# The first stage of a transformer block: x and the condition's weights in larger transfers, the modulation computed ahead of the first transposes

## The chip, the cores and the metric

The kernel runs on one core of one Trainium2 chip. The metric is the time of one execution in device microseconds (us), lower is better. Two more numbers are told apart from it: the span, from the first to the last instruction of one profiled execution, and the time of that same execution, which is a little longer than its span.

## The reference, cut to what matters

One block with adaptive modulation: 2 rows of 2048 tokens, 512 features, 16 heads of 32, hidden size 2048, all in float32. The condition (2 x 512) makes six vectors per row, which shift, scale and gate.

```
mod = silu(condition) @ Wada + bada
sh_a, sc_a, gt_a, sh_m, sc_m, gt_m = split(mod, 6)
xn = layernorm(x) * g1 + be1
xm = xn * (1 + sc_a) + sh_a
x = x + gt_a * attention(xm, Wqkv, Wproj, bproj)       # causal
xn = layernorm(x) * g2 + be2
xm = xn * (1 + sc_m) + sh_m
x = x + gt_m * (gelu(xm @ W1 + b1) @ W2 + b2)
```

## The kernel before, in words

**Stages.** For each of the two rows: a stage that makes q, k and v (class Qkv, pool names qkv0 and qkv1), then attention (attention_phase). The projection of the first row's attention runs in project_phase together with the beginning of the second row's q/k/v stage. The MLP over all tokens ends the kernel. The change edits the beginning of the first row's q/k/v stage, and three methods that both rows use: load_x, and through Qkv.run the order of stats and scaled.

**The q/k/v stage.** A row is cut into 4 groups (g) of 512 tokens, a group into 4 tiles of 128 tokens (MTT = 4). For each group x is loaded (load_x, line 915), each tile's mean and variance are taken by VectorE (stats, L218 bn_stats and L221 bn_aggr), ScalarE takes the square root (L224), VectorE inverts it and makes shift = -mean/std (L225, L226), and ScalarE scales each tile in place (scaled, L964). A pair of tiles (half a group, j = 0 or 1) is then transposed by TensorE (transposed, L214, eight transposes of 128x128 into two PSUM banks), and VectorE (L269) and ScalarE (L274) apply the modulation on the way out into xmT. The products use one level of a seven-product scheme (Strassen's, in the form of Winograd). For each block f of 128 columns of q and k, and then for two blocks of the values, a unit issues the products a(A11), b(S1), a(S2), b(S4), c(A12), a(S3), and, after the first two steps of the next unit, a(A22). Several products add to one PSUM bank, and ScalarE (L1059) or VectorE (L1072, L1078) must copy or subtract a bank's value before the next product is added to it. GpSimd (POOL) makes the sums of weights that the scheme needs (weight_sum L944, value_weight_sums L949), VectorE the sums of tokens (L997). The first block of the first group is done without the scheme (plain: 8 matmuls of 128x512, ps_qk), so that it does not wait for those sums. q and k are split in two parts each (hi on ScalarE L1064, lo minus hi on VectorE L1066, in later groups on POOL) and stored to scratch memory by SyncE (SP, L1031).

**The order around the steps.** Qkv.run counts steps (n, 42 per group); at step 3 it asks for the next group's x if it is not there, at steps 10 to 13 it takes its statistics, at 15 and 25 it scales its tiles in pairs, at 18 and 28 it transposes them, and at 30 it asks for the x after that. From group 1 on, scores of the attention (tile s, with their maxima on VectorE, L498 and L504) are mixed into the steps. A scheduler then orders each engine's instructions; those wrapped in act(), mm() or transpose() keep their program order on their engine, the others may be moved. stats takes a flag keep, which wraps its bn_stats in act(). So a flag here can move other instructions of VectorE and ScalarE too.

**The beginning of the first row** (lines 1360 to 1474). ScalarE issues seven small transfers, cond, g1, be1, g2, be2, b1 and b2, into one tile rows of 44 rows. SP issues x of group 0 (4 transfers of 128x512), the two blocks of Wada for shift and scale (load_wada, 8 transfers of 128x512 into room borrowed from the value tile vv), the q/k weights wqk (4 of 128x2x512) and the value weights wv (4 of 128x2x256). TensorE transposes rows (ps_c), VectorE copies it to cols, ScalarE makes silu of the condition's columns into sc (L1457). modulation(0) is 8 matmuls (ps_mod) of 32 columns of weights each, in four column strips of the array; its columns() adds the bias, brings the result into columns by 4 small matmuls (ps_modt) and copies it to mod; scale_shift makes a1 and c1 from it, with which the transposed tiles are modulated. In the program the first pair of tiles is transposed ahead of modulation(0), the second behind it. ScalarE needs one set of tables for Sqrt and another for Silu, and loads them when it changes from one to the other.

x tiles have 4 buffers; a new x waits until its buffer's last tile is scaled and transposed.

Of the kernel before, what the change touches and what calls it, by code (L numbers as in the profile page):

```python
# [17 lines left out]
P = 128  # L18
# [9 lines left out]
def dit_block_kernel(  # L28
# [106 lines left out]
    first = const.tile([P, 1], F32, tag="first", name="first")  # L135
    nc.scalar.activation(first, eps, AF.Sqrt)

# [760 lines left out]
    class Qkv:  # L898
# [16 lines left out]
        def load_x(self, g):  # L915
            xts = []
            for t in range(MTT):
                xt = self.qp.tile([P, D], F32, tag="x", name="x", bufs=4)
                nc.sync.dma_start(xt, x_rows(self.row.b * NT + g * MTT + t))
                xts.append(xt)  # L920
            self.xts[g] = xts
# [216 lines left out]
        def run(self, hp, also, early=()):  # L1138
# [3 lines left out]
            for g in range(NG):  # L1142
                at = [0]

                def tick():
# [5 lines left out]
                    if g + 1 < NG:  # L1151
                        if n == 3 and g + 1 not in self.xts:
                            self.load_x(g + 1)
                        if 10 <= n < 10 + MTT and g + 1 > row.b:
                            self.stats(g + 1, n - 10)
                        if n in (15, 25):
                            self.scaled(g + 1, n // 25)
                        if n in (18, 28):
                            self.norm(g + 1, n // 28)()
                        sums = {36: S1, 38: S2, 40: S3}  # L1160
                        if n in sums:
                            self.token_sum(g + 1, sums[n])
# [199 lines left out]
    with pool("wada") as wp, pool("qkv0") as qp, pool("hl0") as hp, pool(  # L1362
        "ps_qkv0", bufs=6, space=PSUM
    ) as ps_mm:
        rows = wp.tile([n_rows, P], F32, tag="rows", name="rows")
        for r, n, src in (
            (0, n_cond, cond.rearrange("b (c p) -> (b c) p", p=P)),
# [5 lines left out]
            (r_b2, C, b2.rearrange("(c p) -> c p", p=P)),  # L1373
        ):
            nc.scalar.dma_start(rows[r : r + n, :], src)
        wada_v = Wada.rearrange("(c p) f -> p c f", p=P)
        wada = {}

        def load_wada(s0, s1):
# [6 lines left out]
            for n, s in enumerate((s0, s1)):  # L1386
# [3 lines left out]
                )  # L1390
            for k in range(C):
                for n, s in enumerate((s0, s1)):
                    nc.sync.dma_start(w[:, n, k, :], wada_v[:, k, s * D : (s + 1) * D])
            wada[s0] = w, mr
# [47 lines left out]
        def scale_shift(a, c, r_g, r_be, shift, scale):  # L1442
# [13 lines left out]
        act(  # L1456
            nc.scalar.activation(  # L1457
                sc[:, :, :B], col(0, n_cond).rearrange("p (b c) -> p c b", c=C), AF.Silu
            )
        )  # L1460
# [15 lines left out]
        def also(g, n):  # L1476
# [852 lines left out]
```

## Time and profile before

| | us |
|---|---|
| median of 3 runs | 2249.56 (2248.82 to 2253.02) |
| the profiled execution: its time | 2252.46 |
| its span | 2250.7 |
| TensorE idle within the span | 40.6 |
| start of the first q/k matmul (ps_qk) | 18.28 |
| start of the first product by the scheme (ps_a) | 26.95 |
| granted TensorE clock, mean over the span | 0.999 |

Views used below: the page, the chain that ended last (start, length, engine, tile and line of each piece, in order of time), windows (busy time of each engine in a stretch, granted clock, share of the DMA engines' time, GB/s), and the timeline (start, length, engine, line, operation, tiles, shapes, count; in brackets the idle time before it and what ended it). PE is TensorE's matmuls, PEld its weight loads, DVE VectorE, ACT ScalarE, SPq the issue of transfers on SyncE. A float32 matmul is two records in the trace, a transpose one.

### The profile page before, as it was taken

What the parts mean: (1) busy time and instruction counts of PE and PEld (TensorE: products, weight loads), DVE (VectorE), ACT (ScalarE), POOL (GpSimd) and SP (SyncE); (2) the same over time, 40 slices, a digit from 0 to 9 for tenths busy, and PEclk for the clock granted to TensorE, in tenths of its full rate; (3) what the DMA queues carried; (4) which work ended last, traced back from release to release, by engine and by line L of the source; (5) the groups of instructions that cost most, each with busy time, mean ns of one, the idle gap of its engine ahead of it and who ended that gap; (6) DMA issues with size and microseconds to landing.
All of it is one profiled execution on the core that took longest, in us unless ns stands there. A gap on an engine that the chain in (4) does not pass through costs nothing.

```text
span 2250.7 us, 33467 instructions
## 1 busy us (share of the span) xinstructions
PE 2210.1 (98%) x12057; PEld 1429.4 (64%) x12057; DVE 1537.3 (68%) x3309; ACT 1003.6 (45%) x2012; POOL 1298.3 (58%) x807
## 2 busy tenths in 40 slices
PE   7999999999999999999999999999999999999998
PEld 5887555555543588855555555345787787688687
DVE  4678766777757667777677767663685585576576
ACT  4434555555564253365665556614322422331410
POOL 4253998998983696299989898444105204304210
PEclk9999999999999999999999999999999999999999
DMA  8787142231324799532324113363353354353433
GB/s 274 247 277 193 44 92 70 62 85 48 107 96 135 247 308 321 152 83 67 80 67 104 48 46 131 108 233 127 114 174 131 125 182 147 106 187 126 159 126 109
DMA packets 160510, 311.57 MB, mean 138 GB/s; under 512 B 16544, under 2 KB 48844, under 8 KB 158552
## 3 DMA queue, kind: packets, MB, share of 16 engines
q1 hardware_dynamic: 155488, 285.53, 41.8%
q0 software_dynamic: 4480, 23.36, 2.7%
q8 instruction: 95, 1.56, 0.3%
q14 instruction: 71, 0.58, 0.1%
q10 hardware_dynamic: 376, 0.55, 0.1%
HBM read 229.95 MB, written 87.29 MB: 141 GB/s over the span
## 4 chain that ended last, share of the span: by engine, by line
PE 88%; DVE 4%; POOL 3%; DMA 2%; ACT 1%; issue 1%; SPq 0%; DVEq 0%; ACTq 0%; POOLq 0%
PE ps_a L206 26%; PE st L206 18%; PE ps_b L206 12%; PE o L206 10%; PE s L206 9%; PE ps_c L206 4%; PE sm L206 3%; PE ps_o L206 3%; DVE junk L498 1%; POOL ee L695 1%; PE ps_xt L214 1%; ACT e L670 1%; DVE mx L504 1%; PE ps_o L214 1%; DVE stat L218 1%
## 5 line engine op out<-in xcount | busy, mean ns | idle before, releaser
L670 ACT ACTIVATE e<-st 128x512 f32<-128x512 f32 (+1 forms) x1152 | 575.1, 579 | 362.6 <-PE st L206 319.2
L504 DVE TENSOR_REDUCE mx<-s 128x1 f32<-128x512 f32 x576 | 381.6, 686 | 193.4 <-PE s L206 192.4
L695 POOL TENSOR_TENSOR ee<-ee,e 128x2048 f32<-128x2048 f32 x106 | 485.8, 4583 | 10.4 <-ACT e L670 4.4
L206 PE MATMUL st<-qst,kst 128*128 128x512 f32 (+3 forms) x1280 | 408.8, 386 | 0.0
L206 PE MATMUL s<-kst,qst 128*128 128x512 f32 (+3 forms) x1046 | 380.5, 395 | 6.1 <-DVE mx L504 3.7
L206 PE MATMUL ps_a<-sum,w 128*128 128x256 f32 (+1 forms) x1088 | 328.7, 431 | 0.1
L206 PE MATMUL o<-e,vv 128*32 128x512 f32 (+3 forms) x2560 | 293.2, 537 | 0.3 <-POOL e L682 0.3
L206 PEld LDWEIGHTS st<-qst,kst 128*128 128x128 f32 x1280 | 228.5, 188 | 97.7 <-issue 66.0
L498 DVE CUSTOM_DVE_ANT_0 junk<-s,causal 128x128 bf16<-128x128 f32 (+3 forms) x470 | 220.7, 470 | 61.0 <-PE s L206 47.0
L1797 POOL TENSOR_TENSOR sum<-w 128x256 f32<-128x256 f32 x30 | 22.1, 738 | 395.2 <-PE ps_a L206 263.8
L206 PEld LDWEIGHTS s<-kst,qst 128*128 128x128 f32 x1046 | 194.9, 188 | 71.1 <-DVE mx L504 17.0
L206 PEld LDWEIGHTS ps_a<-sum,w 128*128 128x128 f32 x1088 | 204.5, 190 | 40.1 <-issue 11.4
L695 POOL TENSOR_TENSOR ee<-e 128x2048 f32<-128x2048 f32 x42 | 192.5, 4583 | 43.2 <-ACT e L670 42.3
L206 PEld LDWEIGHTS <-sel 32*128 32x128 bf16 x1152 | 29.5, 91 | 197.0 <-issue 196.1
L2016 ACT ACTIVATE h<-h,cols 128x512 f32<-128x512 f32 x120 | 76.8, 711 | 136.0 <-DVE h L1718 136.0
L504 DVE TENSOR_REDUCE mx<-st 128x1 f32<-128x512 f32 x192 | 131.0, 683 | 0.6
L682 POOL TENSOR_SCALAR_AFFINE_SELECT e<-e 128x512 f32<-128x512 f32 x128 | 83.3, 669 | 67.6 <-ACT e L670 67.5
L206 PE MATMUL st<-fold,sel 32*128 32x512 bf16 (+1 forms) x1152 | 117.5, 372 | 1.3
L206 PEld LDWEIGHTS o<-e,vv 128*32 128x32 f32 x2560 | 59.1, 108 | 92.4 <-issue 73.0
L1718 DVE TENSOR_TENSOR h<-c,ps_b 128x256 f32<-128x256 f32 x90 | 37.9, 421 | 103.5 <-PE ps_b L206 103.0
L1066 POOL TENSOR_TENSOR lo<-lo,hi 128x512 fp32r<-128x512 f32 x32 | 40.6, 1274 | 103.9 <-ACT hi L1064 102.0
L206 PE MATMUL ps_b<-sum,w 128*128 128x256 f32 (+1 forms) x384 | 95.0, 383 | 0.0
(237 smaller groups left out, 3590.2 us busy)
## 6 DMA issues: line engine op xcount, KB each, us to landing
qst<-q SPq DMA_DIRECT2D x128, 256.0 KB
kst<-k SPq DMA_DIRECT2D x128, 256.0 KB
w<-w1d SPq DMA_DIRECT2D x32, 896.0 KB
w<-w2d SPq DMA_DIRECT2D x28, 1024.0 KB
w<-w2d SPq DMA_DIRECT2D x28, 768.0 KB
q<-hi SPq DMA_DIRECT2D x32, 256.0 KB
q<-lo SPq DMA_DIRECT2D x32, 256.0 KB
k<-hi SPq DMA_DIRECT2D x32, 256.0 KB
```

Of the source, the lines that this page charges most:

```text
L206: return tc.keep_in_program_order(nc.tensor.matmul(*args, **kw))
L214: return tc.keep_in_program_order(nc.tensor.transpose(dst, src, ident[:n, :n]))
L218: ins = nc.vector.bn_stats(st, xt)
L498: nc.vector.tensor_tensor_reduce(junk[:, :w], x, causal[:, QB - w :], 1.0, MASKED, ALU.add, ALU.max, m,)
L504: self.vector(nc.vector.tensor_reduce(m, x, axis=AX.X, op=ALU.max))
L670: act(nc.scalar.activation(e4[:, h, :w], sts[h][:, :w], AF.Exp))
L682: nc.gpsimd.affine_select(d, d, pattern=[[0, HC], [1, P]], compare_op=ALU.is_ge, fill=0.0, base=0, channel_multiplier=-1,)
L695: act(nc.gpsimd.tensor_tensor(dst, x, y, ALU.add))
L1066: engine.tensor_tensor(lo, d, hi.bitcast(F32), ALU.subtract)
L1718: act(nc.vector.tensor_tensor(dst, x, y, ALU.add))
L1797: act(engine.tensor_tensor(dst, u, v, op))
L2016: nc.scalar.activation(d[j], d[j], AF.Gelu, bias=col(r_b1 + half * HF + fs[j], 1))
```

## The change

- load_x loads a group's x by two transfers of two tiles each; the buffers become two of two tiles.
- load_wada takes two chunks of 128 rows in one transfer (4 instead of 8), and modulation takes its chunks in the order 0, 1, 2, 3 instead of 0, 2, 1, 3.
- Only cond, g1 and be1 are loaded at the start, into a tile of 16 rows. The other 28 rows are loaded on SP at step 22 of group 0 and transposed into columns at step 20 of group 1.
- The table of Silu is loaded first, ScalarE makes sc straight from the PSUM tile ps_c, and the table of Sqrt comes after it.
- TensorE transposes the identity 6 times before ps_c and 24 times after it, into a tile that nothing reads (busy).
- Both pairs of tiles of group 0 are scaled ahead of modulation(0), both are transposed after it.
- x of group 1 is asked for ahead of the value weights.
- The statistics of group g+1 keep their program order in group 0 of the first row and in group 1 of the second.

```
     first = const.tile([P, 1], F32, tag="first", name="first")
-    nc.scalar.activation(first, eps, AF.Sqrt)
...
-            for t in range(MTT):
-                xt = self.qp.tile([P, D], F32, tag="x", name="x", bufs=4)
-                nc.sync.dma_start(xt, x_rows(self.row.b * NT + g * MTT + t))
-                xts.append(xt)
+            for t in range(0, MTT, 2):
+                xt = self.qp.tile([P, 2, D], F32, tag="x", name="x", bufs=2)
+                t0 = (g * MTT + t) * P
+                nc.sync.dma_start(
+                    xt,
+                    x[self.row.b, t0 : t0 + 2 * P, :].rearrange("(n p) d -> p n d", p=P),
+                )
+                xts += [xt[:, n, :] for n in range(2)]
...
-                            self.stats(g + 1, n - 10)
+                            self.stats(g + 1, n - 10, row.b == g)
...
-            nc.scalar.dma_start(rows[r : r + n, :], src)
+        for r, n, src in parts[:3]:
+            act(nc.scalar.dma_start(rows[0][r : r + n, :], src))
+        act(nc.scalar.activation(first, eps, AF.Silu))
+
+        def load_other_rows():
+            for r, n, src in parts[3:]:
+                nc.sync.dma_start(rows[1][r - r_g2 : r - r_g2 + n, :], src)
+
+        def other_columns():
+            ps = ps_sp.tile([P, n_rows - r_g2], F32, tag="s", name="ps_c")
+            transpose(ps, rows[1])
+            nc.vector.tensor_copy(cols[:, r_g2:n_rows], ps)
...
-            for k in range(C):
+            for k in range(0, C, 2):
                 for n, s in enumerate((s0, s1)):
-                    nc.sync.dma_start(w[:, n, k, :], wada_v[:, k, s * D : (s + 1) * D])
+                    nc.sync.dma_start(
+                        w[:, n, k : k + 2, :], wada_v[:, k : k + 2, s * D : (s + 1) * D]
+                    )
...
         qkv.load_w(nc.sync)
+        qkv.load_x(1)
         qkv.load_wv(hp, nc.sync)
-        ps_c = ps_mm.tile([P, n_rows], F32, tag="mm", name="ps_c")
-        transpose(ps_c, rows)
-        nc.vector.tensor_copy(cols[:, :n_rows], ps_c)
+        ps_w = ps_sp.tile([P, P], F32, tag="s", name="ps_w")
+        def busy(n):
+            for _ in range(n):
+                transpose(ps_w, ident)
+        busy(6)
+        ps_c = ps_sp.tile([P, r_g2], F32, tag="s", name="ps_c")
+        transpose(ps_c, rows[0])
...
-                        kk = half * C // 2 + k
+                        kk = 2 * k + half
...
+        act(
+            nc.scalar.activation(
+                sc[:, :, :B],
+                ps_c[:, :n_cond].rearrange("p (b c) -> p c b", c=C), AF.Silu,
+            )
+        )
+        act(nc.scalar.activation(first, eps, AF.Sqrt))
+        nc.vector.tensor_copy(cols[:, n_cond:r_g2], ps_c[:, n_cond:])
+        busy(24)
         for t in range(MTT):
             qkv.stats(0, t)
-        halves = [qkv.norm(0, 0, True)]
...
+        qkv.scaled(0, 0)
+        qkv.scaled(0, 1)
         picks()
         columns = modulation(0)
+        halves = [qkv.norm(0, 0, True)]
+        columns()
         halves.append(qkv.norm(0, 1, True))
-        columns()
...
             if g == 0 and n == 22:
                 load_wada(2, 5)
+                load_other_rows()
+            elif (g, n) == (1, 20):
+                other_columns()
```

More of the change, by code (lines that the diff above doesn't have):

```diff
@@ L1364, in dit_block_kernel @@
     ) as ps_mm:
-        rows = wp.tile([n_rows, P], F32, tag="rows", name="rows")
-        for r, n, src in (
+        rows = [
+            wp.tile([n, P], F32, tag=f"rows{n}", name="rows")
+            for n in (r_g2, n_rows - r_g2)
+        ]
+        parts = (
             (0, n_cond, cond.rearrange("b (c p) -> (b c) p", p=P)),
@@ L1373, in dit_block_kernel @@
             (r_b2, C, b2.rearrange("(c p) -> c p", p=P)),
-        ):
-            nc.scalar.dma_start(rows[r : r + n, :], src)
+        )
[9 more added lines that the diff above has]
+            nc.vector.tensor_copy(cols[:, r_g2:n_rows], ps)
         wada_v = Wada.rearrange("(c p) f -> p c f", p=P)
@@ L1450, in scale_shift @@
             nc.vector.tensor_tensor(c, c, mod[:, shift], ALU.add)
+        act(
[3 more added lines that the diff above has]
+            )
+        )
+        act(nc.scalar.activation(first, eps, AF.Sqrt))
+        nc.vector.tensor_copy(cols[:, n_cond:r_g2], ps_c[:, n_cond:])
+        busy(24)
         for t in range(MTT):
             qkv.stats(0, t)
-        halves = [qkv.norm(0, 0, True)]
[L1456 to L1460, printed above, removed]
+        qkv.scaled(0, 0)
+        qkv.scaled(0, 1)
         picks()
         columns = modulation(0)
+        halves = [qkv.norm(0, 0, True)]
+        columns()
         halves.append(qkv.norm(0, 1, True))
-        columns()
         scale_shift(a1, c1, r_g1, r_be1, 0, 1)
```

## The prediction

> **What bounds the kernel now.** I read the page first, then the chain that ended last for the first 110 us, then windows over the start, then the timeline around every idle time of TensorE in the two stages that make q, k and v, and last the order in which the two built programs issue their instructions. That order differs in these two stages alone; attention and the MLP have the same instructions in the same order.
>
> ```profile
> span 2250.7 us, 33467 instructions
> ...
> PE 2210.1 (98%) x12057; PEld 1429.4 (64%) x12057; DVE 1537.3 (68%) x3309; ACT 1003.6 (45%) x2012; POOL 1298.3 (58%) x807
> ```
>
> TensorE is busy for 98%, so a microsecond counts only where TensorE waits or runs below its clock. The whole span has 40.6 us of idle TensorE, and the first q/k matmul starts at 18.28. This chain shows why (start, length, what):
>
> ```profile
> 9.90 1.75 PE ps_xt L214 x7
> 11.65 2.96 PE ps_mod L206 x16
> 14.61 1.02 PE ps_xt L214 x8
> 15.63 0.88 PE ps_modt L206 x8
> ...
> 17.23 1.01 DVE xmT L269 x2
> ...
> 18.28 8.85 PE ps_qk L206 x16
> ...
> 35.63 1.73 PE ps_a L206 x8
> ...
> 39.08 0.87 PE ps_xt L214 x8
> ...
> 69.61 1.85 PE ps_mod L206 x16
> ```
>
> Eight transposes take 0.87 at 39.08 (0.11 each), but seven take 1.75 at 9.90 (0.25 each). One modulation takes 1.85 at 69.61 and 2.96 at 11.65. The 16 records of ps_qk take 8.85; eight records of half their width take 1.73, so 16 wide ones should take 16 x 0.43 = 6.9. The windows give reasons (the last three columns are the granted clock, the DMA engines' busy share, GB/s):
>
> ```profile
> 1.90:4.20 2.30, 0.00 (x0) 0.00 (x0) 0.62 (x1) 0.00 (x0) 2.30 (x7) 1.00 0.91 284
> 4.20:8.30 4.10, 0.30 (x1) 0.18 (x1) 3.51 (x16) 1.78 (x3) 1.20 (x3) 1.00 0.91 277
> 8.30:13.60 5.30, 4.17 (x23) 2.35 (x24) 0.00 (x0) 4.42 (x6) 0.00 (x0) 1.00 0.96 334
> 13.60:17.60 4.00, 2.90 (x21) 1.92 (x18) 1.65 (x6) 0.00 (x0) 0.74 (x2) 1.00 1.05 401
> 16.50:18.28 1.78, 0.00 (x1) 0.00 (x1) 1.63 (x7) 0.41 (x1) 1.42 (x3) 1.00 1.06 387
> 19.50:22.80 3.30, 3.30 (x5) 1.35 (x4) 3.16 (x5) 0.30 (x1) 3.22 (x4) 0.50 1.08 366
> ```
>
> First, the transfers run at 284 and 277 GB/s until 8.3 and at 401 after 13.6. Second, TensorE rests from 16.50 to 18.28, and its clock is at 0.50 from 19.50 to 22.80.
>
> ```profile
> 0.81 2.40 SPq L919 DMA_DIRECT2D x<-in_x_dram  x4
> ...
> 4.23 3.75 SPq L1393 DMA_DIRECT2D vv<-in_L_cond_Wada_dram  x8
> ...
> 13.56 0.14 PEld L206 LDWEIGHTS ps_mod<-vv,sc 128*32 128x32 f32 x2 [0.47 <-DMA vv<-in_L_cond_Wada_dram]
> ...
> 26.95 1.03 PE L206 MATMUL ps_a<-xmT,wqk 128*128 128x256 f32 x4
> ...
> 27.76 1.28 ACT L224 ACT_TABLE_LOAD   x1
> ...
> 29.26 0.36 ACT L1059 ACTIVATE lo<-ps_a 128x256 f32<-128x256 f32 x1
> ...
> 29.72 1.10 PE L206 MATMUL ps_a<-t,wqk 128*128 128x256 f32 x4 [0.89 <-POOL wqk L944]
> ...
> 30.93 1.52 ACT L964 ACTIVATE x<-x,shift,rstd 128x512 f32<-128x512 f32 x2 [1.03 <-issue]
> ```
>
> The last weights of the modulation wait for Wada until 13.56, so Wada's landing leads to 18.28. At 29.72 the row blames POOL, but POOL had made that sum long before. This product adds to a bank that ScalarE must copy first: a table load (1.28), rstd and the copy stand before it and end at 29.62.
>
> **The change, part by part.** *Fewer, larger transfers.* Four x and eight Wada transfers of 256 KB become two and four of 512 KB. In the built order each transfer signals one of eight semaphores in turn and its issue waits for the transfer eight before it. That is why four issues spread over 2.40 us and eight over 3.75. With the small rows cut from seven to three ahead of them, nine transfers remain, and only the ninth waits, for a row long landed. Up to 13.6 the windows moved 2.3 x 284 + 4.1 x 277 + 5.3 x 334 = 3.56 MB. At 401 GB/s from 1.9 that is done at 10.8. The bounds are 10.8 and 13.6 (the rate stays as it is); I take 10.8, since the only cause that I find for the low rate is removed.
>
> *Modulation ahead.* Pairing chunks 0 and 1, then 2 and 3, in order of arrival leaves half of the modulation after the last landing: 1.0, as now (13.56 to 14.61), so it ends at 11.8. Then the same chain as now, 14.61 to 18.28 = 3.67: eight transposes beside VectorE's sum, ps_modt, four small VectorE steps, two xmT. The second eight transposes lie beside those small steps. The first ps_qk starts at 15.5, **2.8 earlier** (0 to 2.8).
>
> *TensorE busy.* 30 transposes of the identity cost 30 x 0.11 to 30 x 0.25 = 3.2 to 7.5 us, in time in which TensorE waits for Wada. Without that cover 24 of them, up to 24 x 0.25 = 6.0, would stand ahead of the modulation. They and the shorter rest (16.50 to 18.28 becomes 0.7 + 1.0 less the transposes in it, about 0.9) should keep the clock at 1.00: ps_qk takes 6.9, **1.9 less** (0 to 2.0). The clock did rise after work that began with transposes at 9.20: at 14.61 eight of them took 1.02.
> [...]
>
> *Condition's table first.* Silu comes before the one Sqrt load, so the load at 27.76 goes and the wait at 29.72 with it, 1.1 with its follow-up. What is late next? The order on VectorE is new. stats() of group 1 (and of group 2 in the second row) now keeps its program order, and VectorE issues these bn_stats later. The same happens around them to group 2 in the first row. I follow it three times; XT is the block of eight transposes that needs the scaled x.
>
> (1) XT of group 1, row 0. TensorE reaches it 12 steps of 0.86 after ps_qk, at 10.4. `shift` now stands behind the subtraction of step 11's bank on VectorE, which step 11 releases at 9.5; VectorE gets to it at 9.9 and takes 0.42 and 0.16 (rows below), so `shift` is done at 10.5. Two scalings of 0.76 (1.52 at 30.93) follow, and XT ends at 12.1 + 0.87 = 13.0. Now it ends at 39.95, 13.0 after the first ps_a at 26.95. **Net 0**: the table's gain is eaten here (-1.1 to +1).
>
> (2) XT of group 2, row 0.
>
> ```profile
> 73.20 0.69 DVE L218 BATCH_NORM_STATS2 stat<-x 128x6 f32<-128x512 f32 x1
> ...
> 77.38 0.67 DVE L498 CUSTOM_DVE_ANT_0 junk<-s,causal 128x512 bf16<-128x512 f32 x1
> ...
> 78.48 0.69 DVE L1066 TENSOR_TENSOR lo<-lo,hi 128x512 fp32r<-128x512 f32 x1 [0.33 <-ACT hi L1064]
> ...
> 79.09 0.17 DVE L225 RECIPROCAL rstd<-rstd 128x4 f32<-128x4 f32 x1
> ...
> 79.37 0.16 DVE L226 SCALAR_TENSOR_TENSOR shift<-mv,rstd 128x4 f32<-128x4 f32 x1
> 79.48 0.56 DVE L498 CUSTOM_DVE_ANT_0 junk<-s,causal 128x384 bf16<-128x384 f32 x1
> 79.56 2.23 ACT L964 ACTIVATE x<-x,shift,rstd 128x512 f32<-128x512 f32 x3 [0.64 <-DVE shift L226]
> ...
> 79.97 0.42 DVE L1072 SCALAR_TENSOR_TENSOR lo<-ps_b,lo 128x256 f32<-128x256 f32 x1
> ...
> 80.42 0.33 PE L214 MATMUL ps_xt<-ident,x 128*128 128x128 f32 x1 [1.01 <-ACT x L964]
> ...
> 81.13 0.98 PE L214 MATMUL ps_xt<-ident,x 128*128 128x128 f32 x7 [0.38 <-ACT x L964]
> ```
>
> Now the four bn_stats begin at 73.20, between other work, and `shift` is done at 79.53, before the subtraction at 79.97. In the new order all four come after the junk maximum (0.67 + 0.08, from 75.75 at the earliest): four of 0.67, aggregates 0.35, lo minus hi 0.69, an aggregate, two more maxima (1.0), reciprocal 0.17, the subtraction 0.42, `shift` 0.16. That sums to 75.75 + 6.2 = 81.95. Two scalings of 0.74 and XT's last seven (0.87) end at 84.3 instead of 82.0: **2.3 more** (1.2 if VectorE is not the last to come).
>
> (3) XT of group 2, row 1: the same form.
>
> ```profile
> 827.71 0.23 DVE L226 SCALAR_TENSOR_TENSOR shift<-mv,rstd 128x4 f32<-128x4 f32 x1
> ...
> 828.29 1.51 ACT L964 ACTIVATE x<-x,shift,rstd 128x512 f32<-128x512 f32 x2
> ...
> 829.86 0.98 PE L214 MATMUL ps_xt<-ident,x 128*128 128x128 f32 x7 [0.38 <-ACT x L964]
> ```
>
> By the same steps `shift` moves from 827.7 to about 830.3, and XT's second transpose from 829.86 to 831.9: **2.0 more** (0 to 2.7).
>
> (4) One gain that the diff does not show:
>
> ```profile
> 115.92 0.69 DVE L218 BATCH_NORM_STATS2 stat<-x 128x6 f32<-128x512 f32 x1 [1.57 <-DMA x<-in_x_dram]
> ...
> 117.26 1.92 PE L206 MATMUL ps_mod<-vv,sc 128*32 128x512 f32 x16 [0.95 <-DVE mx L504]
> ```
>
> Here ps_mod waits 0.95 for a maximum that stands behind a bn_stats waiting for x. The new order puts that maximum first: **0.9 less** (0 to 0.95; the pair of x lands later than a single tile, but only the maximum after it waits).
>
> *At nothing.* load_x(1) now stands ahead of load_wv on SP and blocks it until x's tiles are transposed, to about 15. wv is first read by POOL behind 12 weight sums. Behind Wada 4.2 MB (the q/k weights, x and wv) at 401 GB/s are in by 10.8 + 10.5 = 21.3, and those sums cannot begin before 15, so POOL does not wait; if it did, the first value products behind it would. The four other rows cost SP four issues of some 0.35 at step 22, one transpose and a 28-column copy: 0.2, beside idle time of SP. One subtraction on POOL in row 1 moves back behind the weight sums of a piece, and with it one store and two query loads on SP; the stores behind that one wait for POOL there already, so I cost it at 0, at worst one late score block.
>
> **The sum.** 2.8 + 1.9 + 0 - 2.3 - 2.0 + 0.9 = 1.3 less. The profiled execution took 2252.46, 1.76 around its span, so on its footing the result is 2251.2. It lies 2.9 (0.13%) above the median of 2249.56; applied to the median, **2248.3**.
>
> **Rivals.**
> *The transposes are not held up.* If the late statistics cost nothing at the three XT, the gains stay whole: 2.8 + 1.9 + 1.1 + 0.9 = 6.7, so 2242.9. For it: before already waits 1.0 and 0.4 at 80.42 and 81.13, so part of a later `shift` is not new. Against it: the issue order is fixed, and the sums above leave VectorE no idle time.
> *The statistics cost more than the start gains (slower).* VectorE executes in order, and at each XT a bn_stats behind an unfinished subtraction holds `shift`. At the upper ends (1.0 + 3.0 + 2.7, with a maximum more between) the three XT lose about 8.5 against 4.7 + 0.9 gained: 2.9 slower, 2252.5. It decides once the three together exceed 5.6.
> *The clock stays low.* If transposes don't keep it up, ps_qk stays at 8.85: 2248.3 + 1.9 = 2250.2. For it: 1.78 of rest was enough to halve the clock at 19.50.
> *The transfers do not come sooner.* If 300 GB/s is what the memory gives at the start, and not the eight semaphores, 2.8 falls to about 0.3: 2250.8. For it: the DMA engines are 0.91 busy even then. Against it: 0.96 to 1.05 busy gives 334 to 401.
>
> **How the numbers follow.** Forecast 0.42, transposes not held up 0.25, statistics dearer 0.15, clock low 0.08, transfers not sooner 0.10. The likeliest is the forecast, 2248.3, whose own range is 2245.5 to 2251. The range of 2242.5 to 2252.5 takes in the rivals' middles and leaves out the better half of the first and the worse half of the second, together under 0.2. 0.2% is 4.5 us, about what a measurement of this kernel can tell from no change: faster means below 2245.1, slower above 2254.1. Faster takes 0.21 of the first rival and 0.03 of the forecast: 0.24. Slower takes 0.07 of the second and 0.01 of the last: 0.08. The same: 0.68.
>
> **What would show each step.** The last weight load of the first ps_mod waits for Wada until about 10.8, at near 400 GB/s from 4 us on; ps_qk starts near 15.5 and takes 6.9 at a granted clock of 1.00; no table load stands between the two ps_qk evictions and rstd. The XT of group 1 and group 2 in row 0 and of group 2 in row 1 have 1.5 to 4 us of idle TensorE ahead of them, with `shift` and x as releasers. If these are under 1 us, the first rival holds. If Wada lands at 13, or ps_qk takes over 8, the two terms of the start are wrong. I am wrong altogether if attention or the MLP differ by over 1 us.

## The result, and the profile after

The changed kernel is slower, by 0.6%: 2265.4 us (median of 6 runs, 2259.53 to 2270.3) against 2251.06 for the kernel before in the same session (2248.82 to 2253.33); ratio 1.006, 95% interval 1.0041 to 1.0079. The forecast was 2248.3, the range ended at 2252.5, and "slower" had a chance of 0.08.

The profiled execution took 2270.3. It is the slowest of the six, so the losses found in it add up to more (17.6) than the medians differ by (14.3). The page of the changed kernel:

```profile
span 2268.3 us, 33499 instructions
...
PE 2222.8 (98%) x12088; PEld 1440.5 (64%) x12088; DVE 1539.0 (68%) x3310; ACT 1003.2 (44%) x2012; POOL 1297.8 (57%) x807
```

The span is 17.6 longer. TensorE still shows 98%, so this page hides the loss. TensorE's busy time grew by 12.7. The 30 transposes of the identity are 6.1 of it (4.60 for 24 of them, below, and 1.54 for six); the rest is that the same matmuls took longer.

To see where the time went, I compare one kind of instruction in both profiles: ScalarE's CAST from lo to hi, which occurs 62 times in each, spread over both q/k/v stages. The table gives the start of the n-th CAST in before and how much later the same one starts in other kernels (the experiments are explained below; minus is earlier).

| n-th | before | after | n3 | n7 | n8 | n10 | n5 |
|---|---|---|---|---|---|---|---|
| 1 | 34.03 | -4.8 | -3.9 | -3.7 | +1.2 | -4.7 | -3.5 |
| 4 | 43.86 | -0.5 | -3.4 | -0.9 | +0.9 | -2.8 | -3.0 |
| 13 | 101.78 | +2.7 | -2.1 | +0.3 | +1.1 | +0.7 | -0.2 |
| 17 | 122.37 | +1.5 | +1.6 | -1.0 | +0.9 | -0.4 | -0.5 |
| 37 | 802.82 | +3.3 | -0.3 | -2.0 | -1.0 | -2.0 | -2.5 |
| 43 | 832.48 | +10.5 | +8.0 | +0.1 | +6.6 | -1.2 | -1.9 |
| 52 | 881.22 | +10.4 | +6.8 | +0.2 | +6.7 | -1.8 | -1.9 |
| 55 | 908.17 | +17.0 | +6.6 | +5.1 | +12.6 | +3.4 | -1.3 |

After the last row of the table the difference stays within 0.6. The first stage does win 4.8 by 34, but loses 7.5 between 34 and 102 and is 2.7 late there. The two other large losses are in the second row, which the diff hardly seems to touch: 7.2 between 803 and 832, 6.6 between 881 and 908.

**The beginning.** The timeline of the changed kernel (start, length):

```profile
6.18 4.60 PE L213 MATMUL ps_w<-ident 128*128 128x128 f32 x24
10.71 2.80 PE L205 MATMUL ps_mod<-vv,sc 128*32 128x512 f32 x16
...
12.45 0.15 PEld L205 LDWEIGHTS ps_mod<-vv,sc 128*32 128x32 f32 x6 [0.74 <-DMA vv<-in_L_cond_Wada_dram]
...
17.20 7.13 PE L205 MATMUL ps_qk<-xmT,wqk 128*128 128x512 f32 x16 [0.85 <-DVE xmT L268]
```

Wada's last part lands at 12.45 (before 13.56), ps_qk starts 1.1 earlier and takes 7.13 instead of 8.85. Part of these differences is chance: n7 and n12 below keep the start of before, and their ps_qk starts at 18.24 and 19.06 and takes 7.13 in both. The clock column of the windows also reads 1.00 where the trace has no clock record yet, here until 9.83; that the clock was lower until then shows in the transposes of the identity, which follow each other at 0.21 before 9.83 and at 0.11 after it. The windows of the same kernel (TensorE's busy time is the first number behind the length, the granted clock the third from the right):

```profile
1.90:4.20 2.30, 1.40 (x6) 0.99 (x6) 0.00 (x0) 1.49 (x2) 2.30 (x7) 1.00 0.81 284
4.20:8.30 4.10, 2.31 (x11) 2.30 (x12) 3.68 (x15) 1.85 (x4) 1.20 (x3) 1.00 0.94 337
8.30:13.60 5.30, 5.30 (x33) 2.93 (x32) 0.16 (x1) 2.93 (x4) 0.00 (x0) 1.00 1.05 394
...
33.72:37.13 3.41, 1.66 (x9) 1.02 (x8) 1.77 (x6) 2.50 (x6) 3.33 (x5) 1.00 0.95 224
37.13:40.55 3.42, 3.42 (x12) 2.90 (x11) 1.11 (x2) 2.62 (x6) 0.18 (x1) 0.50 1.05 311
78.10:81.51 3.41, 1.33 (x5) 0.82 (x5) 2.27 (x11) 1.69 (x5) 0.00 (x0) 1.00 1.01 220
81.51:84.92 3.41, 3.03 (x12) 2.64 (x12) 0.00 (x0) 3.08 (x6) 0.00 (x0) 0.50 1.05 249
```

The last four rows are the news: after a window in which TensorE was busy for 1.66 or 1.33 of 3.41, the next 3.41 run at half clock. Ahead of the last 3 us, where both kernels end at half clock, the clock records of this execution show it five times, from 37.13, 81.51, 777.83 and 846.09 for 3.41 each and from 907.53 for 6.83: 20.5 us at half clock, which cost 10.2. Before had one such window, 1.7.

**The blocks of transposes (XT)** that the prediction followed:

```profile
36.06 0.33 PE L213 MATMUL ps_xt<-ident,x 128*128 128x128 f32 x1 [1.37 <-ACT x L967]
...
81.31 0.33 PE L213 MATMUL ps_xt<-ident,x 128*128 128x128 f32 x1 [1.71 <-ACT x L967]
...
835.12 0.33 PE L213 MATMUL ps_xt<-ident,x 128*128 128x128 f32 x1 [1.12 <-ACT x L967]
```

**The second row, 803 to 845.** One late instruction goes through five engines:

```profile
809.87 1.28 POOL L1256 TENSOR_TENSOR vv<-vv 128x512 f32<-128x512 f32 x1
...
810.14 4.00 DVE L1000 TENSOR_TENSOR t<-xmT 128x512 f32<-128x512 f32 x1 [1.31 <-PE ps_b L205]
...
818.00 1.13 PE L205 MATMUL ps_a<-wv,t 128*128 128x256 f32 x4 [1.85 <-DVE vv L1137]
...
822.50 0.32 SPq L1034 DMA_DIRECT2D k<-lo  x1
...
831.34 5.41 SPq L1244 DMA_DIRECT2D qst<-in_L_cond_W_dram  x2
...
842.40 1.26 POOL L1256 TENSOR_TENSOR kst<-kst,qst 128x512 f32<-128x512 f32 x1 [11.68 <-DMA k<-hi]
842.98 0.62 ACT L1067 CAST hi<-lo 128x512 fp32r<-128x512 f32 x1 [4.64 <-DMA k<-hi]
...
844.63 1.13 PE L205 MATMUL ps_a<-t,wqk 128*128 128x256 f32 x4 [3.28 <-ACT lo L1062]
```

The same sum in the kernel before:

```profile
806.87 0.88 DVE L997 TENSOR_TENSOR t<-xmT 128x512 f32<-128x512 f32 x1 [0.68 <-PE ps_b L206]
```

VectorE's sum of tokens takes 4.00 instead of 0.88. The subtraction of vv behind it is late, TensorE waits 1.85, and VectorE's work after it is late too, so SyncE issues the store of k's lo part at 822.50 (before 816.17). In SyncE's queue the loads of x and of W2's pieces stand behind this store. GpSimd waits until 842.40 (the row names a store, but what this sum reads are the pieces loaded into kst and qst, the last of them issued from 831.34 to 836.75; in n8 the row names that load); ScalarE's CAST waits for a buffer whose store stands behind those same loads; and TensorE waits 3.28 for ScalarE.

**The second row, 881 to 908:**

```profile
887.10 0.38 SPq L1034 DMA_DIRECT2D k<-hi  x1
...
898.84 4.98 POOL L1069 TENSOR_TENSOR lo<-lo,hi 128x512 fp32r<-128x512 f32 x4
900.16 0.34 SPq L1034 DMA_DIRECT2D k<-lo  x1
900.55 2.55 SPq L359 DMA_DIRECT2D qst<-q  x2
...
908.51 0.77 PE L205 MATMUL s<-kst,qst 128*128 128x512 f32 x1 [4.82 <-issue]
```

The same in the kernel before:

```profile
875.44 0.38 SPq L1031 DMA_DIRECT2D k<-hi  x1
...
878.93 1.27 POOL L1066 TENSOR_TENSOR lo<-lo,hi 128x512 fp32r<-128x512 f32 x1
...
880.23 0.34 SPq L1031 DMA_DIRECT2D k<-lo  x1
880.62 0.92 SPq L360 DMA_DIRECT2D qst<-q  x2
```

SyncE waits between the stores of hi and lo for GpSimd's subtraction: 4.8 from issue to issue in before, 13.1 in after, where the subtraction stands behind all weight sums of a piece. The two query loads behind it are late, and a score block waits 4.82. The row names no releaser; in n8 and n10 below the same wait is put down to the query load.

### The profile page after: what moved, and what is told of

It is laid out like the page before. It is cut to its first block, busy times and chain, and to the rows that moved or that the text cites. A ratio compares the mean times of both kernels' runs of the same rounds, so it can differ in the third digit from the quotient of the medians.

```text
span 2268.3 us, 33499 instructions
## 1 busy us (share of the span) xinstructions
PE 2222.8 (98%) x12088; PEld 1440.5 (64%) x12088; DVE 1539.0 (68%) x3310; ACT 1003.2 (44%) x2012; POOL 1297.8 (57%) x807
## 3 DMA queue, kind: packets, MB, share of 16 engines
q8 instruction: 95, 1.56, 0.3%
## 4 chain that ended last, share of the span: by engine, by line
PE 87%; POOL 5%; DVE 4%; DMA 2%; issue 1%; ACT 1%; SPq 0%; ACTq 0%; DVEq 0%; POOLq 0%
PE ps_a L205 25%; PE st L205 18%; PE ps_b L205 11%; PE o L205 10%; PE s L205 9%; PE ps_c L205 3%; PE sm L205 3%; PE ps_o L205 3%; POOL ee L694 1%; DVE junk L497 1%; PE ps_xt L213 1%; POOL vv L1256 1%; ACT e L669 1%; DVE mx L503 1%; PE ps_o L213 1%
```

## The experiments

Ratios are to the kernel before, with 95% intervals; times are medians.

| kernel | us | ratio (95%) |
|---|---|---|
| after | 2265.40 | 1.0060 (1.0041 to 1.0079) |
| n1_no_keep | 2261.25 | 1.0049 (1.0032 to 1.0066) |
| n2_row1_single | 2266.87 | 1.0073 (1.0058 to 1.0088) |
| n3_row1_undone | 2258.96 | 1.0031 (1.0020 to 1.0043) |
| n4_no_busy | 2265.67 | 1.0061 (1.0037 to 1.0085) |
| n5_gap | 2251.53 | 0.9998 (0.9986 to 1.0010) |
| n6_pool_pinned | 2269.43 | 1.0078 (1.0056 to 1.0101) |
| n7_keep_alone | 2258.45 | 1.0032 (1.0021 to 1.0042) |
| n8_pairs_alone | 2266.33 | 1.0057 (1.0042 to 1.0072) |
| n9_gap_fill | 2251.14 | 0.9997 (0.9989 to 1.0006) |
| n10_after_gap | 2258.46 | 1.0032 (1.0020 to 1.0043) |
| n11_single_transfers | 2252.85 | 1.0001 (0.9992 to 1.0010) |
| n12_before_gap | 2251.15 | 0.9996 (0.9986 to 1.0007) |

n1 to n4, n5 to n8 and n9 to n12 ran on three different chips, on which the kernel before had medians of 2249.82, 2251.40 and 2252.42. Times of different groups can be compared to that extent, the ratios better. Each profile is one execution.

The theory after reading the two traces, theory 1: the loss is made by the order of issue in the second row, where GpSimd's subtraction now stands behind the weight sums. Its rivals: the flag alone (A), the larger x transfers of the second row (B), the clock, shifted by something at the start (C). What n1 to n4 left over gave theory 2 (VectorE's token sum meets GpSimd's sums) and theory 3 (the rule of the clock).

### Undoing the flag and the pairs: n1, n2, n3

n1_no_keep is the changed kernel with

```
-                            self.stats(g + 1, n - 10, row.b == g)
+                            self.stats(g + 1, n - 10)
```

> The changed kernel with one edit undone: the statistics of the next group are no longer held in program order (the flag keep). The pairs of x stay, and with them POOL's order in the second row (one subtraction behind the weight sums). Theory 1 (the loss is made by the order of issue in the second row, and pairs or flag each bring it): 2258 to 2266, the wait of a score block for its queries near 908 stays (3 us or more), and only the wait of the value product near 818 (1.85) goes. Rival A (the flag alone makes the loss): 2250 to 2254, with no wait over 1.5 near 844 and 908.

2261.25. The wait for the queries is there (4.64, up to 897.77), and so is the value product's wait (1.90, up to 811.93), which theory 1 expected to go. What went is 3.0 in the first row (the wait at 36.06 and its half-clock window) and the long wait of GpSimd for W2 (2.24 instead of 11.68), and the stretch from 803 to 832 costs 3.2 here instead of 7.2. Rival A falls: the flag alone does not make the loss.

n2_row1_single is the changed kernel with

```
+            if self.row.b == 0:
...
+            else:
+                for t in range(MTT):
+                    xt = self.qp.tile([P, D], F32, tag="x", name="x", bufs=4)
+                    nc.sync.dma_start(xt, x_rows(self.row.b * NT + g * MTT + t))
+                    xts.append(xt)
```

> The changed kernel, but in the second row x is loaded by single tiles of 256 KB in four buffers again; the flag stays, and so does the order on TensorE, VectorE, ScalarE and POOL; only SyncE's order changes. Theory 1 (order of issue on VectorE, ScalarE and POOL): 2260 to 2268, the waits near 818 and 908 stay within 1 us. Rival B (the larger x transfers of the second row, which wait for two tiles and fill the queues at once): 2250 to 2256, the x issue near 823 comes 5 us earlier and the waits near 844 and 908 go.

2266.87, no better than after; the waits near 818 (1.94) and 908 (4.59) stay. Rival B falls: it isn't the size of the second row's x transfers.

n3_row1_undone has both edits.

> The changed kernel with both undone: single x tiles in the second row, and no flag in either row. POOL's order is then that of before, and the second row's is nearly so. Theory 1: the row-1 loss of about 16 us goes, what is left is the first row's (+1.0 by 776 in the profile after): 2249 to 2254. Rival C (the loss is made by the clock, which something at the start of the first row shifts, so that it halves in later waits whatever the order): 2258 to 2266 with at least three windows of half clock behind 40 us.

2258.96: not theory 1. By its letter this is rival C's outcome: the time lies in its range, and the half clock at 107.02 (6.83) and 816.99 (3.41) makes three windows. But these three cost 5.1, 3.4 of it in the first row, while 8.3 are lost between 803 and 832, where the clock accounts for 1.7. The wait for the queries is gone, as theory 1 says; GpSimd's order is that of before. The timeline of n3:

```profile
806.56 5.21 DVE L1006 TENSOR_TENSOR t<-xmT 128x512 f32<-128x512 f32 x1 [1.30 <-PE ps_b L205]
...
839.89 1.26 POOL L1262 TENSOR_TENSOR kst<-kst,qst 128x512 f32<-128x512 f32 x1 [11.56 <-DMA k<-lo]
```

So theory 1 is only half of the cause. What is common to after, n1, n2, n3 and n4 is one token sum of VectorE that takes 4.0 to 5.2, while GpSimd begins a run of 128x512 sums on vv at most 0.93 from its start (807.49 in n3, 809.87 in after). That is theory 2.

### The transposes of the identity: n4

```
-        busy(6)
-        busy(24)
```

> The changed kernel without the 30 transposes of the identity. If they are what brings the full clock by 9.83: the clock is full only some 3 us after the modulation starts, ps_qk takes 8 to 8.9 instead of 7.13 and starts at the same 17.2, and the time rises by 1 to 2 us against the changed kernel: 2264 to 2268. If they did nothing, ps_qk takes 7.1 as before. If they shift the free-running windows in which the clock is halved (rival C), the time moves by more than 4 us in either direction, with a different set of half-clock windows in the second row.

2265.67, no difference in time, and not the 4 us that rival C asked for. Its ps_qk:

```profile
17.55 7.13 PE L205 MATMUL ps_qk<-xmT,wqk 128*128 128x512 f32 x16 [0.85 <-DVE xmT L268]
```

The clock goes to full at 13.68 instead of 9.83, and the start is 0.35 later (17.55 against 17.20; the eight kernels with the same start and the transposes lie between 16.91 and 17.42), but ps_qk runs at full clock without them. The first reading, 8 to 8.9, was wrong.

### Keeping GpSimd off the token sums: n5, n10, n12

n5_gap is n3 with one instruction more on GpSimd, and the program asks for the sums on vv behind it (step 41 instead of 24). But for this copy every engine's order is that of n3:

```
-                (room_2, 0, 6), (room_1, 16, 24), (room_2, 47, 56), (room_3, 74, 80),
+                (room_2, 0, 6), (room_1, 16, 41), (room_2, 47, 56), (room_3, 74, 80),
...
+            elif (g, n) == (0, 40):
+                junk = qp.tile([P, 1], F32, tag="junk1", name="junk1")
+                act(nc.gpsimd.tensor_copy(junk, qkv.t[S2][:, 0, :1]))
```

> The kernel n3_row1_undone with one instruction more: in the second row GpSimd copies one column of a token sum of group 1 into a scratch tile before its nine 128x512 sums on vv, so that it begins these only when VectorE has made its token sums. No engine's order changes otherwise. Theory 2 (VectorE's token sum takes 5.21 instead of 0.9 because GpSimd's sums run at the same time; the late subtraction behind it holds TensorE, then the store of k on SyncE, then the loads of W2 queued behind that store, then GpSimd for 11.56): the first token sum takes under 1, the waits of TensorE near 813 (2.66) and 840 (2.11) and the half-clock window near 817 (1.7 lost) go, 6.5 less than n3: 2250 to 2254. Rival D (something else slows the token sum, or the W2 loads are late for another reason, DMA bandwidth above all): 2257 to 2261.

2251.53, 7.4 less than n3, as theory 2 has it. The two sets of runs hardly overlap: 2249.53 to 2254.84 (10 runs) against 2253.78 to 2261.73 (8 runs). The timeline of n5:

```profile
806.11 0.69 DVE L1006 TENSOR_TENSOR t<-xmT,t 128x512 f32<-128x512 f32 x1
...
827.56 1.27 POOL L1262 TENSOR_TENSOR kst<-kst,qst 128x512 f32<-128x512 f32 x1 [0.60 <-DMA k<-hi]
```

The first two token sums take 0.85 and 0.69 (the third, behind the point that the copy guards, 1.57). The store of lo is issued at 814.02 instead of 820.11, GpSimd waits 0.60 instead of 11.56, and TensorE's waits near 813 and 840 are gone.

In this execution the copy itself did not have to wait: VectorE had begun its first sum at 804.38, 2.2 earlier than in n3, and the sums had ended before it. That the copy can hold GpSimd back shows in n11 below, which has it too:

```profile
809.01 0.69 DVE L996 TENSOR_TENSOR t<-xmT,t 128x512 f32<-128x512 f32 x1 [0.31 <-PE ps_a L205]
809.77 0.19 POOL L1588 COPY junk<-t 128x1 f32<-128x1 f32 x1 [1.56 <-DVE t L996]
```

GpSimd was ready 0.8 ahead of this sum, waited 1.56 for it, and the sum took 0.69.

n10_after_gap is the whole change with the same instruction.

> The changed kernel whole (pairs, flag), with GpSimd's one added copy that keeps its sums behind VectorE's token sums in the second row. Theory 2: the waits near 816 (1.85) and 841 (3.28) and the half-clock window near 846 (1.7) go, the wait for the queries near 904 (4.82) and its 6.83 us of half clock stay: 6.8 less than the changed kernel, 2256 to 2261. If the three waits are one chain that starts at the token sum, 904 goes too: 2249 to 2253. Rival D (other causes): 2263 to 2268.

2258.46, 6.9 less than after, with 4.71 left at the score block near 896 (the second expectation, one chain for all three waits, falls). The step from n10 to n5 takes off the flag and the second row's pairs, which brings GpSimd's order of before back, and gives the other 6.9. (It also takes the flag off the first row; there the two profiles differ by at most 0.5 at 122 and at 803.) Two causes of about 7 each, by the ratios 6.3 and 7.7.

n12_before_gap is the control, the kernel before with this instruction.

> The kernel before with GpSimd's one added copy alone, a control. In the profile of before VectorE's token sums (806.87 to 810.28) were over as GpSimd's sums began (809.65), so the copy has nothing to undo: 2249 to 2253, no difference from before. If the copy helps in itself (it ends other contention): under 2247.

2251.15: no difference, so the instruction does not help in itself. (The expectation misread one thing: in before the second sum, 808.59 to 810.28, did overlap GpSimd's first by 0.6 and took 1.69; no wait of TensorE near it followed.) In n11 and n12 GpSimd waited at the copy (1.56 and 0.46); in n5, n9 and n10 the sums had ended 0.2 to 0.4 before it. In n9 the second sum began 0.88 ahead of the copy and took 0.69; in n1 it began 0.87 ahead of the run of sums and took 5.13.

### One part alone, on the kernel before: n7, n8

n7_keep_alone is before with the flag, n8_pairs_alone is before with load_x in pairs in both rows (the two hunks of the diff, each alone).

> The kernel before with the flag alone. It moves the same subtraction on GpSimd behind the weight sums of a piece as the whole change does. Theory 1: a wait of a score block of 3 to 5 near 890 and a half-clock window or two behind it, 2255 to 2260. Rival F (the order costs only together with the early start of the first row): 2249 to 2253, no wait over 1.5 there.

2258.45; the flag alone brings the wait at the score block:

```profile
897.92 0.77 PE L206 MATMUL s<-kst,qst 128*128 128x512 f32 x1 [4.64 <-issue]
```

> The kernel before with x in pairs of tiles alone (both rows). It moves the same subtraction on GpSimd. Theory 1: the same wait near 890 and the clock behind it, 2255 to 2260; Wada lands at 13 to 13.6 as before. If larger x transfers alone make the start faster (the prediction's first term), ps_qk starts before 17.5. Rival F: 2249 to 2253, no wait over 1.5 near 890.

2266.33: the pairs alone, without the other edits and their gain, lose as much as the whole change, dearer than expected, since they meet the collision too (a token sum of 5.14):

```profile
813.82 1.93 PE L206 MATMUL ps_a<-wv,t 128*128 128x256 f32 x4 [1.91 <-DVE vv L1138]
...
904.34 0.76 PE L206 MATMUL s<-kst,qst 128*128 128x512 f32 x1 [4.56 <-DMA qst<-q]
```

The pairs don't speed up the start: ps_qk begins at 19.36 there, and at 18.24 to 19.06 in the three kernels with the start of before (before, n7, n12). Rival F falls with both kernels.

### Pinning GpSimd's subtractions: n6

```
-                engine.tensor_tensor(lo, d, hi.bitcast(F32), ALU.subtract)
+                ins = engine.tensor_tensor(lo, d, hi.bitcast(F32), ALU.subtract)
+                if g >= 2:
+                    act(ins)
```

on n1.

> The kernel n1_no_keep with GpSimd's subtractions lo minus hi held in program order, so that they stand between the weight sums instead of behind them. Theory 1 (the score block near 893 to 908 waits for queries, whose loads stand on SyncE behind a store that waits for that subtraction): the wait of 4.64 and the 6.83 us of half clock after it (3.4 lost) go, 8 less than n1: 2252 to 2255. Rival E (the queries are late because of the transfers in pairs, not because of the order): 2259 to 2263, with the wait still over 3.

2269.43, outside both. The wait for the queries shrinks from 4.64 to 1.86, but the pinned order mixes the subtractions otherwise than before did, and a larger wait comes ahead of it:

```profile
893.06 2.08 PE L205 MATMUL ps_a<-t,wqk 128*128 128x256 f32 x4 [6.46 <-ACT lo L1062]
```

The run does not price the order by itself. That price rests on the contrast: the wait of 4.6 to 4.8 is in all seven kernels with the subtraction moved behind the sums (after, n1, n2, n4, n7, n8, n10) and in none of the six with the order of before (before, n3, n5, n9, n11, n12). In the profiles GpSimd issues one sequence in the seven and another in the six, the added copy left out, and the two differ in the place of this subtraction alone. But the seven also share moves on ScalarE and VectorE between 848 and 872 (two CASTs, the two subtractions of lo behind them on VectorE, one tile's statistics). So the contrast prices this bundle of moves; that the subtraction is what holds the queries is read from the chain of the two profiles above and was not isolated by a run. Why both the flag and the pairs make the scheduler move it is not shown.

### The clock: n9

n9_gap_fill is n5 with six transposes of the identity into the bank of XT of group 2 in the first row, ahead of its own:

```
+            for _ in range(fill if cc == 0 else 0):
+                transpose(ps[:, 0, :P], ident)
```

> The kernel n5_gap with six transposes of the identity ahead of the transposes of group 2 in the first row, where TensorE waits 0.98, 0.80 and 0.38 close together. Theory 3 (the clock is set for windows of 3.413 us on a fixed grid, to half where TensorE was idle for more than half of the window before, 1.71): the idle time of that window falls from 1.8 or more to about 1.2, the half-clock window near 79 does not come, 1.7 less: 2248 to 2251.5. Rival G (the clock does not follow idle time in this way, or transposes do not count as work): the half-clock window near 79 to 82 stays, 2250 to 2253.

The windows of n5:

```profile
75.34:78.75 3.41, 1.58 (x6) 0.81 (x5) 2.56 (x11) 2.52 (x6) 0.00 (x0) 1.00 1.00 217
78.75:82.16 3.41, 3.08 (x11) 2.81 (x12) 0.00 (x0) 2.91 (x6) 0.00 (x0) 0.50 1.04 228
106.06:109.48 3.42, 1.88 (x8) 0.99 (x6) 1.29 (x2) 1.42 (x4) 0.00 (x0) 1.00 0.17 64
```

and of n9:

```profile
75.35:78.76 3.41, 2.24 (x12) 1.67 (x13) 2.10 (x11) 2.52 (x6) 0.00 (x0) 1.00 1.05 210
78.76:82.18 3.42, 3.42 (x19) 2.84 (x20) 1.22 (x3) 3.42 (x7) 0.00 (x0) 1.00 1.05 221
106.07:109.48 3.41, 1.40 (x6) 0.89 (x6) 1.81 (x3) 1.83 (x5) 0.00 (x0) 1.00 0.21 77
109.48:112.90 3.42, 3.42 (x9) 2.71 (x9) 0.60 (x2) 0.00 (x0) 0.00 (x0) 0.50 0.93 269
```

Theory 3 holds for the window that it named: TensorE busy 2.24 instead of 1.58, and full clock behind it. The time does not tell the two apart (2251.14 against 2251.53, inside both ranges). In the profiled execution the gain is lost again at the next wait: with the work shifted in the grid, a window that had 1.88 of busy time in n5 came to 1.40 and halved the clock behind it. Rival G falls by the windows, in one execution each.

### The size of the transfers: n11

n11_single_transfers is n5 with x by single tiles in both rows and Wada in eight transfers:

```
-            for k in range(0, C, 2):
+            for k in range(C):
                 for n, s in enumerate((s0, s1)):
-                    nc.sync.dma_start(
-                        w[:, n, k : k + 2, :], wada_v[:, k : k + 2, s * D : (s + 1) * D]
-                    )
+                    nc.sync.dma_start(w[:, n, k, :], wada_v[:, k, s * D : (s + 1) * D])
```

> The kernel n5_gap with single transfers of 256 KB again for x and Wada in both rows; three small rows first, table first, transposes of the identity and modulation ahead stay. It prices the transfers alone. If they are what brings Wada sooner (12.45 against 13.56): the last weights of ps_mod wait until 13.3 or later, ps_qk starts at 18 or later, 0.8 to 1.0 more than n5: 2251 to 2254. If the three small rows and the order bring it: ps_qk starts at 17.1 to 17.6 and the time is that of n5 within 0.5: 2250 to 2253.

2252.85, within the noise of n5. The timeline:

```profile
2.68 4.06 SPq L1407 DMA_DIRECT2D vv<-in_L_cond_Wada_dram  x8
...
12.26 0.14 PEld L205 LDWEIGHTS ps_mod<-vv,sc 128*32 128x32 f32 x2 [0.54 <-DMA vv<-in_L_cond_Wada_dram]
...
16.97 7.13 PE L205 MATMUL ps_qk<-xmT,wqk 128*128 128x512 f32 x16 [0.85 <-DVE xmT L268]
```

Eight issues again spread over 4.06, and yet Wada lands at 12.26 and ps_qk starts at 16.97, both within what the eight kernels with large transfers and the same start show (12.16 to 12.67, 16.91 to 17.42). The larger transfers bring nothing here; the lead of the start comes from the other edits.

## Why the prediction was wrong, by its own steps

- **Fewer, larger transfers, 2.8 earlier.** Measured 1.1 in these two profiles (0.8 to 2.2 over the profiles of either start), and not from that cause. The volume was right (by 12.45 the windows of after moved 3.67 MB, 3.56 were reckoned); the rate was not 401 GB/s from 1.9 on but 284, 337 and 394 in the three windows. The waits named are in the trace of before (SyncE's issues of x and Wada wait 0.7, 0.2 and 1.0 for the landing of an earlier transfer), but as the cause, issues held up by eight semaphores in turn, they fall with n11, where eight issues still spread over 4.06 and Wada lands at 12.26. Four small transfers fewer ahead of the rest remain as the likely source (Wada's issue begins at 4.23 in before, 1.81 in after, 2.68 in n11); that was not tried alone.
- **TensorE busy, 1.9 less in ps_qk.** The size fits these two profiles (1.7), the cause was wrong, and the size is partly luck. n4 has it without the transposes. The rest ahead of ps_qk is 0.85 instead of 1.78, because the second eight transposes now lie behind ps_modt; in none of the ten kernels with this rest did the clock drop there. But a rest of 1.78 does not always halve it: n7 and n12 rest 1.77 and 1.78, and their ps_qk takes 7.13. The 8.85 was one execution of before, and the prediction took it for the kernel. It had seen 1.78 of rest halve the clock and named it only in a rival. On the third rival's condition, that transposes don't keep the clock up: this trace speaks against it. The clock of after goes to full at 9.83, inside the 24 transposes from 6.18 to 10.78, with nothing but transposes before it, and over all profiles it goes to full at 7.78 to 11.72 with the transposes of the identity (nine kernels) and at 12.64 to 15.28 without (five).
- **Condition's table.** Right: no table load stands there (in after the loads begin at 2.08 and 6.48 and take 1.28 each), and TensorE's waits of 0.89 and 0.22 behind it are gone. The first ps_a starts 2.8 earlier (24.17), by the two terms above alone; the first CAST behind the table's place is 4.8 earlier, 2.0 more (1.1 was forecast).
- **(1) XT of group 1, row 0, net 0.** The order was right, the wait was 1.37 and 0.38 and ate the table's gain; but the half-clock window behind it cost 1.7 more. Of 4.8 gained at 34, 0.5 is left at 44.
- **(2) XT of group 2, row 0, 2.3 more.** The n-th CASTs give 3.3 (-0.6 at the tenth, 77.83 in before, to +2.7): 1.2 of additional idle time, the prediction's lower bound in size (VectorE's `shift` was the last to come, as in its main case), and 1.7 for the clock.
- **(3) XT of group 2, row 1, 2.0 more.** 0.6 more idle time (1.12 against 0.56). ScalarE's scaling does wait for `shift` there (0.63), as forecast, but `shift` has fallen back by 0.9 against TensorE's products ahead of it, where 2.6 was reckoned.
- **(4) The wait of 0.95 at ps_mod.** Gone, as worked out: the lead moves by 1.2 between the 13th and the 17th CAST.
- **At nothing.** This is the step that failed, and with the next one it makes the kernel slower. "One subtraction on POOL in row 1 moves back ... I cost it at 0, at worst one late score block." The worst case came, with the clock on top: 4.82 of wait and 6.83 at half clock, which overlap, 6.6 in all. I had argued that SyncE waited for POOL there already; it did, but the two query loads behind that store went from 880.62 to 900.55, 9.5 more than the 10.4 by which all was late, and the scores had no slack for that.
- **What no step had.** A token sum of VectorE within 0.9 of a run of GpSimd sums (7.2 with what followed; 3.2 and 3.4 in n1 and n4, where GpSimd's wait for W2 was 2.24 and 3.29). And the clock: I counted idle time at its face value, while in 29 of 31 windows of 3.41 (below) more than 1.71 of it was followed by half clock, which costs up to 1.7 more for each 3.41.
- **What is left without both losses.** n5 is as fast as before (0.9998), not faster. Its profile leads by 3.5 at the first CAST and by 1.3 at the 55th; 1.7 of the 3.5 is before's half clock in ps_qk.

The rival on the other side ("the statistics cost more than the start gains") had the sign but not the mechanism: the three XT cost 8.5 in it. In the first row it was near: 7.5 were lost around the two XT there, 3.4 of it through the clock, and the start's gain was gone by 102. But the 13.8 that then make the kernel slower come from two waits outside the XT. By its end, 2252.5, it was 13 short.

## What to carry to other kernels

Where a scheduler orders instructions, an edit of a shared helper must be followed to every place that uses it, on every queue: the loads behind a store that waits for a moved instruction are the first to ask about. An idle time of TensorE is not priced by its length alone; several that fell into one window of 3.41 us and filled more than half of it cost up to 1.7 more for each 3.41 at half clock here, behind 29 of 31 such windows. And a narrow miss between VectorE and GpSimd cost 3 to 8 here, where in six of seven kernels the token sum, by its free length, would have ended some 0.2 us ahead of GpSimd's run; one instruction of dependence made it safe. Last, a half-clock window seen in one profile can be chance: n7 and n12 have the rest of before ahead of ps_qk without it. It belongs in a forecast only with a chance of its own.

## What the runs showed of the hardware

**The clock follows windows.** Ahead of the end of the span, half-clock stretches last 3.41 or 6.83 (in after four records of 3.412 to 3.414 and one of 6.827, in before one of 3.413). I cut the 14 profiles (before, after, n1 to n12) into windows of 3.413 from the first full-clock record of each, and took as idle what has neither a matmul nor a weight load. There are 9150 windows at full clock. Of the 31 with more than 1.71 of idle time, half a window, 29 were followed by half clock (the least 1.72; the exceptions 1.85 and 1.89); of the other 9119 one was (1.11, at the start of n8; the largest without, 1.70). So more than half a window of idle time was enough in 29 of 31. That the grid is fixed shows in after: its full-clock records ahead of the five half-clock ones, 27.31, 40.96, 692.91, 64.85 and 58.03 long, are 8, 12, 203, 19 and 17 times 3.413. It shows in the control n12 too, where the rest ahead of ps_qk is 1.78 as in before, but falls on two windows:

```profile
14.64:18.05 3.41, 2.64 (x21) 1.82 (x16) 1.32 (x6) 0.00 (x0) 0.53 (x1) 1.00 1.06 390
18.05:21.47 3.42, 2.41 (x6) 1.22 (x7) 3.31 (x6) 1.94 (x4) 3.27 (x5) 1.00 1.09 356
```

No half clock follows, ps_qk takes 7.13 from 19.06, and the span is 2248.6. In before it fell into one:

```profile
16.06:19.47 3.41, 1.64 (x7) 1.03 (x8) 2.82 (x9) 1.60 (x4) 1.94 (x4) 1.00 1.07 376
19.47:22.88 3.41, 3.41 (x5) 1.35 (x4) 3.27 (x5) 0.33 (x1) 3.33 (x4) 0.50 1.08 365
```

I take this to be part of why the same program varies by some us from run to run; the six runs of after go with the clock's mean, from 0.995 at 2270.3 to 0.997 at 2259.53 and 2260.11. The difference of 0.002 is worth about 4.5 of the 10.8 between them, so it is not all.

**VectorE against GpSimd.** The token sum (128x512) takes 0.69 free (in n11 at 807.29, 808.01 and 809.01). Where it began 0.9 before GpSimd's run of 128x512 sums, or 0.3 behind its start, it took 4.00 to 5.21 in seven kernels (after, n1, n2, n3, n4, n6, n8), some three to four sums of GpSimd, whose first two took 1.26 to 1.28 each there. In six of the seven VectorE's sum had, by the records, started first; in after GpSimd's had (809.87 against 810.14). In before and n7 it took 1.69 and 1.50 instead, with the same 0.9 to 1.1 between the two starts, and GpSimd's first sum 1.76 instead of 1.28. What decides between the two stays open.
